# Two wide steps of the last block's quantizer put on VectorE, with a new table of due times, in a one-core perceiver kernel

## The chip, the cores and the metric

The kernel runs on one core of a Trainium2 chip. The metric is the device time of one execution in microseconds; 1745.08 us is the median of three runs of the kernel before the change. The engines are named as in the profile: PE (TensorE; its weight loads are PEld), DVE (VectorE), ACT (ScalarE), POOL (GpSimd) and SP (SyncE, which issues all DMAs here).

## What is computed

Two perceiver layers on 128 batches of 32 latent tokens of width 256, with a context of 257 tokens per batch, in f32:

```python
x = x + cross_attention(ctx, layernorm(x))            # 257 context tokens
x = x + gated_scan(layernorm(x))                      # 16 states x 512 channels, over 32 tokens
x = x + ternary_mlp(layernorm(x))                     # 256 -> 1024 -> 256, weights -1, 0, 1
x = x + focused_linear_attention(layernorm(x), ctx)   # 16 heads
x = x + latent_attention(layernorm(x))                # 16 heads, decay by distance
x = x + bitlinear_mlp(layernorm(x))                   # the quantized MLP
```

The last line is the one that the change touches. Both of its layers quantize their input by rows to 8 bits:

```python
def activation_quant(x):
    scale = 127.0 / clip(max(abs(x), axis=-1), EPS, None)
    return clip(round(x * scale), -128, 127) / scale
def bitlinear(x, w, b):
    xn = rmsnorm(x)
    return einsum('bsi,oi->bso', activation_quant(xn), weight_quant(w)) + b
# the MLP: bitlinear(gelu(bitlinear(x, w1, b1)), w2, b2), 256 -> 1024 -> 256
```

## The kernel before

**Tiles and stages.** Four batches make a group: 128 rows (4 x 32 tokens) of 256 columns, one tile `x`. The 32 groups are dealt into nine blocks, `BLOCKS = (2, 4, 4, 4, 4, 4, 4, 4, 2)` (line 1507). For each block the code records, in this order: per group the context stage (`context_group`, line 993: cross attention, then keys and values of the linear attention: `pkey`, `ku`, `ks`, `pval`, `vf`, `pk`); for the block the scan stage (`scan_block`, line 1155); and per group the latent stage (`latent_group`, line 1469: `mlp`, `linear`, `attention`, `quantized_mlp`).

**The scan stage** works on up to four groups at once (128 x 512) or two (128 x 256, in the first and the last block). It has four chunks of channels. A chunk begins with two projections `pproj` on PE, an ACT step `some` and a DVE step `pproj<-pproj,b_in,dl`; then come 16 states, each with an exponential `a` on ACT, a scan `h<-a,pproj` on DVE, and a weighted sum `acc` on DVE or, for some of the states, `h` and `some` on POOL. When the four chunks are done, `pout` on PE and `x<-pout,x` on DVE end the stage for each group.

**The quantized MLP** (line 1439) of a group: normalize (`xn`), row maximum `amax`, first quantizer, transpose (`pqT`, copied by ACT to `qT`), product `phq` with w1, scale and bias on DVE into `hq` (two halves), GELU on ACT, row maximum `amax` of `hq` on DVE, squares on ACT (`junk`, sum to `msq`), second quantizer, transpose, product `poq` with w2, and `x<-poq,dq,x` on DVE; SP writes the rows out.

**The quantizer** (line 1409) forms `rms` (a scale step and a power on POOL), `top`, its reciprocal and `qm` on DVE and the factor `dq` on POOL. Then come two steps on the whole tile: the scaling, which multiplies by `qm` and adds a large constant that rounds to an integer, in place (`hq<-hq,qm` or `xn<-xn,qm`), and the rounding, which takes the constant off again and writes bf16 (`q<-hq` or `q<-xn`). In the second quantizer (n = HID = 1024) both steps run on POOL, lines 1424 to 1427. In the first (n = 256) the scaling runs on DVE and the rounding on POOL.

**What sets the order.** Nothing runs where the code stands. A `Recorder` (line 267) notes every operation with the engines that it could run on; `order` (line 403) then plans all of them, and `trace` (line 566) issues them in the planned order, so nearly every instruction of the program has line 575 in the profile, and tiles tell them apart. Each group of operations has a pair in the table `DUE` (line 1510, 251 pairs): the due times of its first and last operation, in units of one block; `R.part()` and `R.begin()` start a new pair. The planner walks through time with the estimated costs of `ns_of` (line 42). Of the operations that can start within `WINDOW` ns of the first, it takes on each engine the one that is due first. `AHEAD` puts DMAs earlier, `SOONER` puts readers of PSUM earlier, `HORIZON` limits how far ahead of the earliest due operation a new buffer may be opened, and `PRICE` weighs the engines where an operation may run on several (copies, casts, `relu`). The planner also assumes that a POOL operation on tensors and a DVE operation of some forms (a wide `tensor_scalar` outside PSUM among them) don't run at the same time:

```python
            locks = engine == "gpsimd" and len(ins) > 0
            ...
                locks = len(tensors) > 1 if two else fast and len(tensors) > 0 and n > 64
```

Where PE has a planned gap of over 600 ns, `keep_busy` (line 553) puts in filler matmuls (`onesb,identb`, line 562), whose results are not used.

Of the kernel before, what the change touches and what calls it, by code (L numbers as in the profile page):

```python
# [12 lines left out]
ALU = mybir.AluOpType  # L13
# [3 lines left out]
P = 128  # L17
D = 256
# [569 lines left out]


GAP, FILL = 600.0, 0.7  # L590
PRICE = {"tensor": 0.0, "vector": 20.786091, "scalar": 1.959533, "gpsimd": 3.101899, "sync": 0.0}
WINDOW = 13.816
SOONER = 0.066
AHEAD = 0.777235
HORIZON = 1.581593


@with_exitstack
def perceiver_kernel(ctx: ExitStack, tc: tile.TileContext, t: dict, out: bass.AP):
# [806 lines left out]
        R.vector.tensor_tensor(xg, py[:, 0:D], xg, ALU.add)  # L1406


    def quantize(h, n, ms, k, amax, gamma):

        rms = tiny("rms", [P, 2])
        R.gpsimd.tensor_scalar(rms, ms.to_broadcast([P, 2]), k, 1e-6, ALU.mult, ALU.add)
        R.gpsimd.tensor_tensor(rms, rms, halves[:, 1:3, 0], ALU.pow)
        top = tiny("top", [P, 1])
        R.vector.tensor_scalar(top, rms[:, 0:1], 1e-5, amax, ALU.mult, ALU.max)
        m = tiny("qm", [P, 1])
        R.vector.reciprocal(m, top)
        R.vector.tensor_scalar(m, m, 127.0, None, ALU.mult)  # L1420
        worth = tiny("dq", [P, 1])
        R.gpsimd.tensor_scalar(worth, top, rms[:, 1:2], gamma, ALU.mult, ALU.mult)

        engine = R.gpsimd if n == HID else R.vector
        engine.tensor_scalar(h, h, m, ROUND, ALU.mult, ALU.add)
        q = (t2k if n == HID else t1k)([P, n], f"q{n}", BF16)
        R.gpsimd.tensor_scalar(q, h, -ROUND, 1.0, ALU.add, ALU.mult)
        return q, worth

    def transposed_ints(q, n):  # L1430
# [5 lines left out]
        R.scalar.copy(qT, pt[:, 0:n])  # L1436
        return qT

    def quantized_mlp(xg):
        xn, mv, r = norm(xg)  # L1440
        R.gpsimd.tensor_tensor(xg, xg, b2, ALU.add)
        amax = tiny("amax", [P, 1])
# [1 line left out]

        msq = tiny("msq", [P, 1])
        R.gpsimd.tensor_scalar(msq, mv[:, 1:2], r, r, ALU.mult, ALU.mult)
        q, dq = quantize(xn, D, msq, 1.0, amax, g1)
        qT = transposed_ints(q, D)
        hid = t4k([P, HID], "hq")
        for k in range(2):  # L1450
# [8 lines left out]
        junk = t2k([P, HID], "junk", BF16)  # L1459
        msq2 = tiny("msq2", [P, 1])  # L1460
        R.scalar.activation(junk, hid, AF.Square, accum_out=msq2)
        q2, dq2 = quantize(hid, HID, msq2, 1.0 / HID, amax2, g2)
        qT2 = transposed_ints(q2, HID)
        po = bank("poq")
        with R.together():
            accumulate(po[:, 0:D], [(qT2[:, c * P : (c + 1) * P], w2[:, c, :]) for c in range(8)])
        R.vector.scalar_tensor_tensor(xg, po[:, 0:D], dq2, xg, ALU.mult, ALU.add)

    def latent_group(xg, kvc, rows_out):
        mlp(xg)  # L1470
        R.part()
        linear(xg, kvc)
        R.part()
        attention(xg)
        R.part()
        quantized_mlp(xg)
        R.sync.dma_start(rows_out, xg)


# [1 line left out]
    for i, size in enumerate(BLOCKS):  # L1481
# [13 lines left out]
        for g in range(size):  # L1495
            n = n0 + g
            R.begin("l")
            latent_group(x[g], kvc[g], out[n * P : (n + 1) * P, :])
        n0 += size
    R.trace(tc)  # L1500

# [6 lines left out]


DUE = (  # L1510
    (-1.0, -0.7651), (0.1, 0.598373), (-1.116179, -1.019716), (-0.267211, 0.164717),
    (0.144, 0.184841), (0.213655, 0.218655), (0.394, 0.426463), (0.439863, 0.48282),
    (0.532341, 1.432341), (0.5, 0.607991), (0.607991, 0.869596), (0.869596, 1.1312),
    (1.1312, 1.392805), (1.39625, 1.657855), (1.65441, 1.696152), (1.574, 1.896954),
    (1.896954, 2.121576), (2.121576, 2.355619), (2.406412, 2.76275), (1.72375, 2.046704),
    (2.046704, 2.271326), (2.271326, 2.556162), (2.556162, 2.995629), (0.61878, 0.663036),
    (0.663036, 0.769121), (0.894, 0.920109), (0.927339, 0.989925), (1.167588, 1.172588),
    (1.172588, 1.241114), (1.394, 1.432573), (1.432573, 1.525039), (1.502252, 1.54223),
    (1.614935, 1.874087), (1.968546, 2.13324), (2.13324, 2.392392), (2.392392, 2.651545),
    (2.651415, 2.69787), (2.574, 2.896954), (2.896954, 3.121576), (3.222754, 3.50759),  # L1520
    (3.406412, 3.76275), (2.72375, 3.047077), (3.047077, 3.271959), (3.271959, 3.557125),
    (3.557125, 3.913875), (2.8735, 3.196454), (3.196454, 3.421076), (3.421076, 3.705912),
    (3.705912, 4.06225), (3.02325, 3.346204), (3.346204, 3.482831), (3.570826, 3.855662),
    (3.855662, 4.212), (1.644, 1.68374), (1.68374, 1.779), (1.979937, 2.019938),
    (2.019938, 2.115825), (2.140124, 2.178549), (2.178549, 2.270656), (2.424535, 2.429535),
    (2.429535, 2.55775), (2.500109, 2.615044), (2.615044, 2.874196), (2.874087, 3.13324),
    (3.13324, 3.392392), (3.392392, 3.651545), (3.651545, 3.698), (3.574, 3.896954),
    (3.896954, 4.121576), (4.121576, 4.406412), (4.406412, 4.76275), (3.72375, 4.046704),
    (4.046704, 4.271326), (4.264978, 4.556162), (4.556162, 4.9125), (3.8735, 4.196454),
    (4.196454, 4.421076), (4.421076, 4.705912), (4.631254, 4.987592), (4.02325, 4.609143),  # L1530
    (4.32519, 4.570826), (4.515235, 4.800071), (4.855662, 5.212), (2.636204, 2.676672),
    (2.676672, 2.773677), (2.886204, 2.925944), (2.925944, 3.021204), (3.147975, 3.187715),
    (3.187715, 3.282975), (3.386204, 3.431648), (3.396284, 3.505216), (3.422175, 3.53711),
    (3.536298, 3.79545), (3.79545, 4.054603), (4.054603, 4.313755), (4.392392, 4.651545),
    (4.651545, 4.698), (4.574, 4.896954), (4.896954, 5.121576), (5.121576, 5.406412),
    (5.406412, 5.76275), (4.72375, 5.046704), (5.046704, 5.271326), (5.271326, 5.556162),
    (5.556162, 5.9125), (4.702612, 5.025566), (5.196454, 5.421076), (5.421076, 5.705912),
    (5.705912, 6.06225), (5.02325, 5.346204), (5.346204, 5.570826), (5.570826, 5.855662),
    (5.855662, 6.212), (3.636204, 3.66871), (3.66871, 3.746629), (3.886204, 3.925944),
    (3.925944, 4.021204), (4.136204, 4.175136), (4.081628, 4.26846), (4.386204, 4.425944),  # L1540
    (4.425944, 4.521204), (4.521056, 4.554079), (4.627973, 4.890743), (4.874087, 5.156898),
    (5.13324, 5.392392), (5.392392, 5.651545), (5.651545, 5.698), (5.574, 5.896954),
    (5.896954, 6.121576), (6.121576, 6.406412), (6.406412, 6.76275), (5.722633, 6.045587),
    (6.045587, 6.270209), (6.270209, 6.555045), (6.555045, 6.911383), (5.8735, 6.196454),
    (6.196454, 6.421076), (6.421076, 6.705912), (6.705912, 7.06225), (6.02325, 6.346204),
    (6.301902, 6.526524), (6.570826, 6.855662), (6.855662, 7.212), (4.636204, 4.690083),
    (4.675944, 4.771204), (4.886204, 4.927641), (4.927641, 5.02697), (5.144, 5.201758),
    (5.201758, 5.340209), (5.394, 5.431974), (5.431974, 5.523), (5.5, 5.614935),
    (5.614935, 5.874087), (5.874087, 6.13324), (6.13324, 6.392392), (6.392392, 6.651545),
    (6.651545, 6.656545), (6.562991, 7.045242), (6.896954, 7.121576), (7.149964, 7.4348),  # L1550
    (7.406412, 7.76275), (6.72375, 7.046704), (7.046704, 7.271326), (7.271326, 7.556162),
    (7.518889, 7.875227), (6.8735, 7.196454), (7.196454, 7.446346), (7.421076, 7.705912),
    (7.705912, 8.06225), (7.02325, 7.346204), (7.346204, 7.570826), (7.53102, 7.815856),
    (7.855662, 8.212), (5.644, 5.684109), (5.684109, 5.780254), (5.894, 5.934222),
    (5.934222, 6.030635), (6.144, 6.163717), (6.183398, 6.277838), (6.394, 6.433837),
    (6.433837, 6.529331), (6.5, 6.614935), (6.614935, 6.874087), (6.874087, 7.13324),
    (7.13324, 7.392392), (7.392392, 7.651545), (7.651545, 7.698), (7.574, 7.904724),
    (7.896954, 8.121576), (8.121576, 8.406412), (8.406412, 8.76275), (7.72375, 8.046704),
    (8.046704, 8.271326), (8.271326, 8.556162), (8.556162, 8.9125), (7.941126, 8.26408),
    (8.196454, 8.482611), (8.421076, 8.705912), (8.701924, 9.058262), (8.02325, 8.251634),  # L1560
    (8.231279, 8.289197), (8.575174, 8.956992), (8.790837, 9.147175), (6.67874, 6.682632),
    (6.682632, 6.756779), (6.894, 6.93374), (6.93374, 7.029), (7.144, 7.18372),
    (7.18372, 7.278932), (7.422476, 7.462216), (7.462216, 7.557476), (7.501224, 7.553756),
    (7.553756, 7.685065), (7.685065, 7.816374), (7.860101, 7.991409), (7.947682, 8.078991),
    (7.995258, 8.100224), (8.130098, 8.453052), (8.393585, 8.746432), (8.618207, 8.903043),
    (8.903043, 9.259381), (8.369442, 8.664825), (8.664825, 8.870271), (8.870271, 9.13079),
    (9.13079, 9.456707), (8.222592, 8.545546), (8.582878, 8.8075), (8.802406, 9.087242),
    (9.092336, 9.39624), (8.380895, 8.732628), (8.732628, 8.95725), (8.95725, 9.242086),
    (9.242086, 9.598424), (7.644, 7.682997), (7.682997, 7.776475), (7.894, 7.93374),
    (7.93374, 8.029), (8.027527, 8.076377), (8.124824, 8.181667), (8.165022, 8.314484),  # L1570
    (8.366433, 8.49925), (8.732164, 8.864981), (8.847172, 8.866054), (8.489793, 8.799099),
    (8.733373, 8.957995), (9.049952, 9.177105), (8.969544, 9.442262), (8.255137, 8.578091),
    (8.559023, 8.723782), (8.443238, 8.947841), (8.98058, 9.391686),
)


# [75 lines left out]
```

## Time and profile before

| | |
|---|---|
| three runs, us | 1745.08, 1747.30, 1744.87; median 1745.08 |
| the profiled execution, us | 1747.35 |
| its span, first to last instruction, us | 1745.60 |
| mean granted clock | 0.987 |
| instructions | 45752 |
| PE filler matmuls, by the built program | 172 |

The profile shows one execution. Instructions are grouped by tiles (buffer numbers left out, output ahead of the arrow); the columns are the busy time of the group and the mean time of one, then the idle time of the engine just before them and what ended it. A view by stage gives the busy time of each engine between two times. The chain of waits goes back from the last instruction, at each step to what released it.

### The profile page before, as it was taken

The page shows a single profiled execution, that of the slowest core. Times are in us where ns is not written, and L with a number is a line of the kernel's source. Part 1 is how long each engine was busy: PE and PEld are TensorE (multiplying, and loading weights), DVE is VectorE, ACT ScalarE, POOL GpSimd, SP SyncE. Part 2 cuts the span into 40 slices and gives each one's busy share as a digit, 9 for nine tenths or more (in the row PEclk, how much of TensorE's full clock was granted, in tenths as well). Part 3 has the DMA queues.
Part 4 walks back from the last instruction along what each step waited for, and adds up shares of the span by engine and source line. Part 5 has one row for each costly group of instructions (what it writes and reads, how often), then busy time and mean ns, then how long its engine had stood idle before and what let it go on. Part 6 is the DMA issues. An engine that isn't in the chain of part 4 may idle for free.

```text
span 1745.6 us, 45752 instructions
## 1 busy us (share of the span) xinstructions
PE 1657.3 (95%) x17523; PEld 1203.7 (69%) x17591; DVE 1508.2 (86%) x2956; ACT 1426.8 (82%) x3495; POOL 1356.6 (78%) x2145
## 2 busy tenths in 40 slices
PE   8999999999999999999999999999999988888996
PEld 5777777776776777767777677776777665656663
DVE  5479689989988999988999799979999899988866
ACT  3677698889987999879887989888888898777665
POOL 4766758678776988778788779867888799878887
PEclk9999999999999999999999999999999999999998
DMA  7312000111000011001110021001110000000000
GB/s 221 107 45 86 29 29 29 45 41 32 10 29 29 8 64 38 29 2 41 35 35 29 8 62 41 29 2 35 41 35 29 4 23 1 7 1 2 8 8 19
DMA packets 44762, 59.74 MB, mean 34 GB/s; under 512 B 8704, under 2 KB 27008, under 8 KB 44544
## 3 DMA queue, kind: packets, MB, share of 16 engines
q1 hardware_dynamic: 44544, 56.81, 10.1%
q8 instruction: 139, 2.28, 0.6%
q14 instruction: 79, 0.65, 0.1%
HBM read 52.32 MB, written 4.19 MB: 32 GB/s over the span
## 4 chain that ended last, share of the span: by engine, by line
PE 39%; DVE 28%; ACT 14%; POOL 13%; issue 4%; DMA 0%; DVEq 0%; POOLq 0%; ACTq 0%
DVE h L575 13%; PE pval L575 6%; DVE acc L575 6%; PE pkey L575 6%; PE pproj L575 4%; ACT a L575 3%; PE pT L575 3%; POOL ku L575 2%; POOL rstd L575 2%; ACT ks L575 2%; PE pqa L575 2%; PE pmlp L575 2%; ACT L575 2%; PE pk L575 2%; DVE st L575 2%
## 5 line engine op out<-in xcount | busy, mean ns | idle before, releaser
L575 DVE TENSOR_TENSOR_SCAN h<-a,pproj 128x512 f32<-128x512 f32 (+1 forms) x576 | 613.3, 1086 | 22.4 <-ACT a L575 17.6
L575 ACT ACTIVATE a<-dl,a_neg 128x496 f32<-128x496 f32 (+1 forms) x576 | 366.8, 664 | 71.3 <-DVE h L575 68.4
L575 DVE SCALAR_TENSOR_TENSOR acc<-h,w_st,acc 128x512 f32<-128x512 f32 (+1 forms) x436 | 299.5, 687 | 0.6
L575 PE MATMUL pval<-wkv,cT 128*128 128x256 f32 x1024 | 245.5, 386 | 1.4 <-DVE y L575 1.3
L575 PE MATMUL pkey<-wkv,cT 128*128 128x256 f32 x1024 | 238.1, 386 | 0.0
L575 ACT ACTIVATE ks<-ku 128x256 f32<-128x256 f32 x512 | 209.0, 415 | 16.8 <-POOL ku L575 15.5
L575 PEld LDWEIGHTS pkey<-wkv,cT 128*128 128x128 f32 x1024 | 189.3, 190 | 38.0 <-issue 14.9
L575 PEld LDWEIGHTS pval<-wkv,cT 128*128 128x128 f32 x1024 | 188.9, 191 | 31.4 <-issue 2.8
L575 POOL TENSOR_TENSOR ku<-ku,e 128x512 f32<-128x512 f32 x128 | 162.7, 1281 | 33.9 <-ACT ku L575 28.3
L575 POOL TENSOR_TENSOR ku<-ks,ku 128x512 f32<-128x512 f32 x128 | 165.4, 1300 | 18.7 <-ACT ks L575 17.8
L575 POOL TENSOR_TENSOR kn<-kn,halves 128x4 f32<-128x4 f32 x128 | 131.1, 1026 | 24.4 <-ACT ks L575 23.4
L575 POOL TENSOR_TENSOR rstd<-rstd,halves 128x1 f32<-128x1 f32 x224 | 125.8, 565 | 7.3
L575 ACT ACTIVATE vf<-pval,kf 128x256 f32<-128x256 f32 x256 | 107.4, 472 | 23.2 <-PE pval L575 15.5
L575 ACT ACT_TABLE_LOAD x95 | 121.9, 1283 | 1.7
L575 PE MATMUL pproj<-xTs,w_in 128*128 128x512 f32 (+1 forms) x288 | 122.4, 552 | 0.3
L575 POOL TENSOR_SCALAR rstd<-mv 128x1 f32<-128x1 f32 x224 | 45.2, 202 | 96.6 <-DVE mv L575 73.2
L575 POOL TENSOR_TENSOR some<-some,h 128x512 f32<-128x512 f32 (+1 forms) x104 | 115.1, 1107 | 2.8
L575 PE MATMUL pmlp<-w_pr,hT 128*128 128x256 f32 x512 | 116.7, 381 | 0.0
L575 PEld LDWEIGHTS pmlp<-w_pr,hT 128*128 128x128 f32 x512 | 95.6, 190 | 13.8 <-issue 0.8
L575 ACT ACTIVATION_READ_ACCUMULATOR ks<-ku 128x1 f32 x512 | 100.6, 196 | 0.0
L575 POOL TENSOR_SCALAR h<-h,w_st 128x512 f32<-128x512 f32 (+1 forms) x104 | 65.3, 630 | 40.7 <-DVE h L575 35.5
L575 PE MATMUL ph<-w_fc,x 128*128 128x512 bf16 x350 | 89.2, 379 | 5.3 <-ACT ku L575 1.4
(291 smaller groups left out, 3883.7 us busy)
## 6 DMA issues: line engine op xcount, KB each, us to landing
cx<-in_ctx_dram SPq DMA_DIRECT2D x64, 512.0 KB
x<-in_x_dram SPq DMA_DIRECT2D x32, 128.0 KB
cr<-in_ctx_dram SPq DMA_DIRECT2D x128, 32.0 KB
out_dram<-x SPq DMA_DIRECT2D x32, 128.0 KB
vlz<-vl SPq DMA_DIRECT2D x128, 1.1 KB
w_in<-in_w_inT_dram SPq DMA_DIRECT2D x1, 1024.0 KB
raw_fc<-in_w_fcT_dram SPq DMA_DIRECT2D x2, 512.0 KB
raw_pr<-in_w_prT_dram SPq DMA_DIRECT2D x2, 512.0 KB
```

Source lines behind the costliest of these rows:

```text
L575: ins = getattr(engine, name)(*(traced(a) for a in args), **{k: traced(v) for k, v in kw.items()}).ins
```

## The change

The last block's two groups run the scaling and the rounding of their second quantizer on DVE instead of POOL; the first quantizer and all other blocks stay as they were. The five numbers of the planner and all but 2 of the 251 pairs of `DUE` change (their starts by 0.03 of a block in the median). The diff without the rest of the table:

```diff
-PRICE = {"tensor": 0.0, "vector": 20.786091, "scalar": 1.959533, "gpsimd": 3.101899, "sync": 0.0}
-WINDOW = 13.816
-SOONER = 0.066
-AHEAD = 0.777235
-HORIZON = 1.581593
+PRICE = {"tensor": 0.0, "vector": 28.013093, "scalar": 4.356996, "gpsimd": 3.720234, "sync": 0.0}
+WINDOW = 13.821085
+SOONER = 0.0675
+AHEAD = 0.744939
+HORIZON = 1.665209
...
-    def quantize(h, n, ms, k, amax, gamma):
+    def quantize(h, n, ms, k, amax, gamma, late):
...
-        engine = R.gpsimd if n == HID else R.vector
+        wide = R.vector if late else R.gpsimd
+        engine = wide if n == HID else R.vector
         engine.tensor_scalar(h, h, m, ROUND, ALU.mult, ALU.add)
         q = (t2k if n == HID else t1k)([P, n], f"q{n}", BF16)
-        R.gpsimd.tensor_scalar(q, h, -ROUND, 1.0, ALU.add, ALU.mult)
+        engine = wide if n == HID else R.gpsimd
+        engine.tensor_scalar(q, h, -ROUND, 1.0, ALU.add, ALU.mult)
...
-            latent_group(x[g], kvc[g], out[n * P : (n + 1) * P, :])
+            latent_group(x[g], kvc[g], out[n * P : (n + 1) * P, :], i == len(BLOCKS) - 1)
...
 DUE = (
-    (-1.0, -0.7651), (0.1, 0.598373), (-1.116179, -1.019716), (-0.267211, 0.164717),
-    (0.144, 0.184841), (0.213655, 0.218655), (0.394, 0.426463), (0.439863, 0.48282),
+    (-1.233024, -0.335498), (0.019828, 0.480193), (-1.629912, -0.869437), (-0.837897, -0.738361),
+    (-0.093681, -0.088914), (-0.021839, -0.017211), (0.306149, 0.488484), (0.39917, 0.543159),
...
```

`late` is handed down through `latent_group` and `quantized_mlp`. In the built program the work stays nearly the same and its order changes everywhere: four wide steps move from POOL to DVE, 11 casts of `x<-xT` from ACT to POOL, and the fillers go from 172 to 168. At the start, SP issues the first group's `x`, `cx` and `cr` ahead of the weights `wv`, `w_in` and `w_gate`, where they stood behind them.

## The prediction

> **What bounds the kernel now.** I read the page first, then the busy time by stage, then the chain of waits of the last 32 us, and last the rows of the moved steps. Busy shares, from the page:
>
> ```profile
> PE 1657.3 (95%) x17523; PEld 1203.7 (69%) x17591; DVE 1508.2 (86%) x2956; ACT 1426.8 (82%) x3495; POOL 1356.6 (78%) x2145
> DVE   5479689989988999988999799979999899988866
> ```
>
> Four engines work most of the time, so no single sum sets the span. DVE is nearly full from the seventh slice to the thirty-seventh and loose at both ends. Cut at the first scan (98.9 us), at the start of the last one (1622.2) and at the last `x<-pout` (1640.0):
>
> ```profile
> 0.00:98.90 98.90, 93.18 (x790) 69.26 (x791) 43.00 (x114) 49.77 (x161) 57.72 (x108) 0.97 0.48 146
> 98.90:1622.20 1523.30, 1464.62 (x15389) 1064.94 (x15448) 1377.45 (x2590) 1299.05 (x3181) 1202.54 (x1867) 0.99 0.09 29
> 1640.00:1745.60 105.60, 83.66 (x1150) 57.99 (x1154) 71.59 (x208) 67.22 (x132) 83.34 (x149) 0.92 0.04 13
> ```
>
> Columns: window, its length, then busy PE, PEld, DVE, ACT, POOL, clock, DMA. The reader is to see three regimes. The front is PE's (93 of 99 us). The middle is DVE's: 1377.45 of 1523.30, 90.4%. In the end no engine is full, and POOL is the busiest (83.34 of 105.60). The last chain says what the end waits for:
>
> ```profile
> 1729.68 1.10 POOL hq L575
> 1730.78 0.32 POOL dq L575
> 1731.11 1.09 POOL hq L575
> ...
> 1732.56 1.05 POOL q L575
> 1733.60 0.67 POOL rms L575
> 1734.28 1.04 POOL q L575
> 1735.36 1.03 PE pqT L575 x8
> ```
>
> From 1714.09 to 1735.36 that chain hardly leaves POOL: several groups are in their quantizers at once, and their small `rms` and `dq` steps queue between 1 us wide steps.
>
> **The moved steps.** Of 32 groups only the last block's two change engine; that is two scalings `hq<-hq,qm` and two roundings `q<-hq`.
>
> ```profile
> L575 POOL TENSOR_SCALAR hq<-hq,qm x32: 1111/1118/1249, 372.7 to 1735.6; 128x1024 f32<-128x1024 f32 x32
> L575 POOL TENSOR_SCALAR q<-hq x32: 1040/1047/1052, 374.3 to 1736.8; 128x1024 bf16<-128x1024 f32 x32
> L575 DVE TENSOR_SCALAR neg_w<-raw_w,thr x4: 726/746/1768, 133.9 to 165.8; 128x1024 f32<-128x1024 f32 x4
> L575 DVE TENSOR_SCALAR w_out<-w_out x1: 686/686/686, 28.3 to 28.3; 128x1024 f32<-128x1024 f32 x1
> ```
>
> POOL loses 2 x (1.118 + 1.047) = 4.33 us. DVE has no row for either step. The nearest for the scaling is neg_w (same shape, one pointer scalar), 0.746; for the rounding w_out (no pointer, but f32 out instead of bf16), 0.686. So DVE gains 2 x 1.432 = 2.86 us, and one pair is 0.73 us shorter in its own chain.
>
> The relief has a catch in the neg_w row: its maximum is 1.768. That one started at 165.81 while POOL's `ku<-ks,ku` ran, 1.0 us over the median. The `ku` step, begun 0.08 us after an earlier neg_w, took 1.798 us where its group's mean is 1.300: 0.50 more. So either engine's wide step can delay the other. Best case: the steps run side by side and POOL is relieved of all 4.33. By the row, each DVE step costs POOL 0.50: 4.33 - 4 x 0.50 = 2.33. Worst: POOL's relief is hidden by other work and the 2.86 lie on the path, +2.9. I take -2.3, since that row is the same shape beside a wide POOL step, as here.
>
> The Trainium skill speaks against the change here ("SBUF — State Buffer", section "SBUF: two separate sides"): VectorE in a two-port mode and GpSimd lock one port pair for a whole instruction, the loser blocks. As an estimate from it, POOL would lose the whole DVE time of 2.86, and the relief would be 1.47, not 2.33. The two delays above show its direction, not its full length.
>
> **The new table.** All but 2 of its 251 pairs change, so the order of the whole kernel moves. The instructions hardly do: compared by engine and tile, 11 casts `x<-xT` go from ACT (0.405 each) to POOL (0.397), so ACT -4.5 and POOL +4.4; filler matmuls go from 172 to 168; the ACT table loads stay 96. POOL's total is then level (+4.4 - 4.3).
>
> To see what the new order does, I summed each engine's instructions in either built order up to a mark, each at its group's mean busy time in this trace:
>
> ```
> DVE work, us              before   after
> ahead of the first scan     42.0    46.5
> between first and last    1381.4  1373.8
> behind the last scan        84.8    90.8
> behind the last x<-pout     68.2    77.1
> behind the last x<-pya      17.2    22.7
> other engines: ACT behind the last a 76.7 -> 82.0
> POOL behind the last x<-x,s 76.7 -> 81.8; PE behind the last pout 79.5 -> 88.3
> ```
>
> *Front.* SP issues x, cx and cr ahead of wv, w_in and w_gate (1.75 MB), three issues of some 0.5 us earlier. The first context transposes and scores now stand on PE in the stretch where before ran fillers while DVE worked through `sp_y`. But PE's work ahead of the first projection is 86.0 -> 87.4, and it was busy 93 of 99 us. I take 0, with 5 us off as the end: the pieces of the chain that move there are `pT` 0.43, `pq` 1.71, `pcT` 1.02 + 0.87 and `psc` 1.01 us, which stood on it from 23 to 35 us. No loss: of the moved weights wv is first used at 45 us, the others at 92. What counts is that 4.5 us of DVE work slip ahead of the first scan, where DVE idled.
>
> *Middle.* DVE has 7.6 us less between first and last scan. At 90.4% that is 8.4 us.
>
> *End.* More stands behind the last scan on every engine: DVE +6.0, of which 2.9 are the moved steps. From 1622.2 to the end took 123.4 us. If the stretch is set by dependences, the work fits into the idle time: 0. If DVE's share stays as it was, it grows to 123.4 x 90.8/84.8 = 132.1: +8.7. PE has 30 fillers there instead of 12, at a clock that was 0.79 from 1714 on; I count nothing for that. POOL's load gives a similar +7 (81.8/76.7 of 105.6). I take the middle, +4.4.
>
> Sum: -8.4 + 4.4 - 2.3 = -6.3 us. The profiled execution took 1747.35 (span 1745.60, 1.75 around it), the median of three runs is 1745.08, so this execution is 2.3 us slow. On its own time the sum gives 1741.0; on the median 1738.8. I forecast **1739**.
>
> Ends of the sum: -5 - 8.4 + 0 - 4.3 = -17.7, so 1727; and -8.4 + 8.7 + 2.9 = +3.2, so 1748.
>
> **Rivals.**
> *The end takes back what the middle gives.* The work is only pushed past the last scan: -8.4 + 8.7 - 2.3 = -2.0, time 1743. For it: POOL's 79% in the end, and its solid chain. Against: DVE is only 68% busy there (71.59 of 105.60), and these groups were late because they waited. Within 0.2% of 1745.08 (3.5 us, about what a measurement of this kernel can tell from no change).
>
> *Slower: the block starts lose their cover.* Each block begins with projections that wait for the previous stage; DVE then waits for ACT's `some`:
>
> ```profile
> L575 DVE SCALAR_TENSOR_TENSOR pproj<-pproj,b_in,dl 128x512 f32<-128x512 f32 x28 | 21.1, 752 | 36.8 <-ACT some L575 36.7
> ```
>
> With the two-group blocks that is 43.7 us. What DVE can do there is what stands between the previous scan and this `pproj`. Summed over the eight later blocks, that cover falls from 72.9 to 64.6 us in the new order (10.4 to 2.3 at the sixth block alone). If every lost microsecond becomes idle, +8.3, and the end pays its +8.7 too: -8.4 + 8.7 + 8.3 = +8.6, with the relief hidden; time 1754. It decides once the idle time before `pproj` grows by 9.8 us (-6.3 + 9.8 = +3.5), or by 5.5 where the end pays in full. Against it: at four of the eight starts the wait was under 0.3 us, with covers of 6.4 to 16.3; at the other four it was 6 to 10 us with covers of 5.5 to 10.4. So cover is only part of it.
>
> *The change does not do what it says:* DVE's steps hold POOL up so that the relief is gone or reversed. Price: +2.3 to +5.2 on the forecast, 1741 to 1744. It shows as wide steps of 1.5 us or more.
>
> **Chances.** Forecast, with its neighbours to 1741.6: 0.60. End takes it back, or the locked steps, within 0.2%: 0.16. Slower by over 0.2%: 0.24, mostly lost cover. The range runs from 1729 to 1754: it takes in nearly all down to the lower end of the sum, and the slower rival, and leaves out some 2 in 10.
>
> **What would show it.** Front: first scan near 98.9 us or up to 4 earlier. Middle: last scan starting near 1614 rather than 1622.2, DVE busy about 1374 between the two. Steps: four DVE rows 128x1024 of 0.7 to 0.8 us; 1.2 or more means they meet POOL. End: last `x<-pout` near 1633, the time from there to the end 103 to 108 us (105.6 before), and POOL no longer solid from 1714 to 1735. It is wrong if the last scan starts no earlier than 1619, or if the stretch behind it grows by more than 8 us; and the slower rival is right if the idle time before `pproj` passes 53 us.

## The result, and the profile after

| | before | after |
|---|---|---|
| median, us | 1744.97 (1743.05 to 1747.30, 4 runs) | 1716.75 (1713.78 to 1719.02, 4 runs) |
| ratio | | 0.9837 [0.9817, 0.9857] |
| the profiled execution, us | 1747.35 | 1715.90 |
| its span, us | 1745.60 | 1714.20 |
| mean granted clock | 0.987 | 0.996 |

The change made the kernel faster by 28.2 us. The forecast was 1739 and the range ran from 1729 to 1754: the sign was right, the size far too small. Blocks are numbered from 0 to 8 from here on.

The changed kernel's page, the row of busy times and the row of DVE in 40 slices:

```profile
PE 1650.3 (96%) x17587; PEld 1200.9 (70%) x17587; DVE 1501.8 (88%) x2960; ACT 1422.8 (83%) x3484; POOL 1362.6 (79%) x2152
DVE  5389699988997997959998997979999899999777
```

DVE has four instructions more (the moved steps) and yet 6.4 us less busy time; its last slices read 99999777, where they read 99888866. The stretches of the changed kernel, cut at the same events (first scan 96.5, start of the last scan 1590.3, last `x<-pout` 1606.7); columns as before: window, length, busy PE, PEld, DVE, ACT, POOL, clock, DMA:

```profile
0.00:96.50 96.50, 91.33 (x820) 68.27 (x824) 48.50 (x119) 50.83 (x161) 61.29 (x108) 1.00 0.54 161
96.50:1590.30 1493.80, 1455.50 (x15264) 1058.83 (x15260) 1358.92 (x2575) 1289.02 (x3153) 1201.18 (x1869) 1.00 0.09 29
1606.70:1714.20 107.50, 87.92 (x1244) 61.33 (x1242) 79.91 (x227) 73.59 (x143) 86.52 (x151) 0.98 0.04 13
```

The reader is to see that nearly all of the gain stands in the second row: 1523.30 us became 1493.80. DVE's work there fell by 18.5 us (1377.45 to 1358.92), its idle time by 11.0 (145.85 to 134.88). Up to the first scan 2.4 us were won, although DVE does 5.5 us more there (43.00 to 48.50). From the start of the last scan to the end hardly anything changed (123.4 and 123.9 us).

The moved steps, rows of the changed kernel; min/median/max duration in ns, first and last start:

```profile
L575 POOL TENSOR_SCALAR hq<-hq,qm x30: 1111/1117/1131, 358.0 to 1705.3; 128x1024 f32<-128x1024 f32 x30
L575 POOL TENSOR_SCALAR q<-hq x30: 1042/1046/1355, 359.2 to 1706.6; 128x1024 bf16<-128x1024 f32 x30
L575 DVE TENSOR_SCALAR hq<-hq,qm x2: 735/978/1221, 1700.4 to 1704.5; 128x1024 f32<-128x1024 f32 x2
L575 DVE TENSOR_SCALAR q<-hq x2: 684/1069/1454, 1703.5 to 1705.6; 128x1024 bf16<-128x1024 f32 x2
```

Two of the four took 0.735 and 0.684 us, the other two 1.221 and 1.454. The end of the changed kernel's chain of waits (start, length, what):

```profile
1700.37 1.06 ACT hq L575
1701.46 1.15 ACT junk L575 x2
1702.61 0.91 ACT qT L575
1703.56 1.05 PE poq L575 x8
1704.61 0.46 PE pqT L575 x8
1705.09 1.02 ACT qT L575
1706.16 1.05 PE poq L575 x8
```

From 1693.5 us on no POOL step is left in it (further ahead, from 1682 us, it still runs through POOL); where the old chain went through POOL's `hq` and `q` of 1.1 us, it now goes from ACT to PE and back. And DVE's wait for `some` at the starts of the chunks, by its two rows in the changed kernel, is 28.9 + 2.8 = 31.7 us instead of 43.7:

```profile
L575 DVE SCALAR_TENSOR_TENSOR pproj<-pproj,b_in,dl 128x512 f32<-128x512 f32 x28 | 21.1, 752 | 28.9 <-ACT some L575 28.9
L575 DVE SCALAR_TENSOR_TENSOR pproj<-pproj,b_in,dl 128x256 f32<-128x256 f32 x8 | 3.9, 482 | 2.8 <-ACT some L575 2.8
```

### The profile page after: what moved, and what is told of

Its sections match the earlier page's. It is cut to its first block, busy times and chain, and to the rows that moved or that the text cites. A ratio compares the mean times of both kernels' runs of the same rounds, so it can differ in the third digit from the quotient of the medians.

```text
span 1714.2 us, 45797 instructions
## 1 busy us (share of the span) xinstructions
PE 1650.3 (96%) x17587; PEld 1200.9 (70%) x17587; DVE 1501.8 (88%) x2960; ACT 1422.8 (83%) x3484; POOL 1362.6 (79%) x2152
## 4 chain that ended last, share of the span: by engine, by line
PE 48%; DVE 24%; ACT 15%; POOL 10%; issue 3%; DMA 0%; DVEq 0%; POOLq 0%; ACTq 0%; SPq 0%
DVE h L575 10%; PE pkey L575 7%; PE pproj L575 7%; PE pval L575 6%; DVE acc L575 5%; PE pT L575 3%; PE pmlp L575 3%; PE pqa L575 3%; POOL ku L575 3%; ACT a L575 2%; PE pk L575 2%; ACT ks L575 2%; ACT L575 2%; PE pka L575 2%; PE pcT L575 2%
```

## The experiments

The theory after the result: the moved steps are worth some 3 us; the rest is the new order, and it wins at the places where one stage hands over to the next, not by the amount of work. The rivals: the gain is spread over all blocks; it needs the whole new table; or it is the last part alone. Most of the kernels below issue one plan's order up to a mark and the other plan's order from there:

```diff
-        for i in self.order():
+        for i in self.spliced():
...
+        head = first[: ends[CUT - 1] + 1]
...
+        rest = [i for i in second if i not in done]
```

`first` and `second` are the two full plans, each made with its own table and its own five numbers. Of `rest`, the first operation whose inputs are issued and whose buffers are free is taken. `ends` are the `x<-pout` steps: the 2nd ends block 0's scan stage, the 26th block 6's; the 28th is the second of block 7's four. (The expectations call it the end of the eighth block's scan stage; the 30th is that.) All ratios are against runs of the kernel before on the same chip; a gain in us is the ratio's distance from 1 times 1745.

**The steps alone.** The changed kernel with the old table and numbers:

```diff
-PRICE = {"tensor": 0.0, "vector": 28.013093, "scalar": 4.356996, "gpsimd": 3.720234, "sync": 0.0}
+PRICE = {"tensor": 0.0, "vector": 20.786091, "scalar": 1.959533, "gpsimd": 3.101899, "sync": 0.0}
...
 DUE = (
-    (-1.233024, -0.335498), (0.019828, 0.480193), (-1.629912, -0.869437), (-0.837897, -0.738361),
+    (-1.0, -0.7651), (0.1, 0.598373), (-1.116179, -1.019716), (-0.267211, 0.164717),
```

> The four wide steps of the last block on DVE, with the table and the planner's numbers of before; the order is that of before up to the last few instructions. Theory A (the gain is the new order's, made where block 0 and the last block run): 1743 to 1745 us, the relief of POOL worth 0 to 2 us. Theory B (the relief of POOL at the end is a good part of it): 1740 or less. Theory C (the steps lock each other out and cost): 1746 or more. Of before's 32.0 us from the last x<-pya to the end, A expects 30 to 32, B under 29.

Measured: 0.9983 [0.9974, 0.9991], 3.0 us [1.6, 4.5] faster, between theories A (0 to 2) and B (5 or more). The time from the last `x<-pya` to the end went from 31.6 to 28.4 us, as B expected. The four DVE steps took 0.816, 0.694, 0.754 and 0.685, together 2.95 us; only the first met a wide POOL step, for 0.27 us.

**The table alone.** The changed kernel with the steps back on POOL:

```diff
-            latent_group(x[g], kvc[g], out[n * P : (n + 1) * P, :], i == len(BLOCKS) - 1)
+            latent_group(x[g], kvc[g], out[n * P : (n + 1) * P, :], False)
```

> The new table and numbers, all wide steps on POOL as before. Theory A: 1716 to 1719 us, last scan start near 1590 us as in after. Theory B: 1721 or more, and the stretch behind the last x<-pout longer than after's 107 us by 4 or more.

Measured: 0.9851 [0.9837, 0.9865], 26.0 us, so 1719 by the ratio (its median of 1721.85 stands beside 1747.17 for the kernel before on that chip): theory A, at its slow end. The stretch behind the last `x<-pout` took 110.4 us, 2.9 more than after the change. Nine tenths of the gain are the order's, and 3.0 + 26.0 is about the whole, 28.4 by its ratio. The profiled execution of this kernel, whose lines are shown below, was the fastest of its four: 1717.41 us at clock 0.997, where the others took 1721.8 to 1723.0 at 0.991 or 0.992.

**The new order up to the end of block 0's scans** (`FIRST` new, `SECOND` old, `CUT = 2`).

> Order spliced: the new plan's order up to the second x<-pout (end of block 0's scan stage), then all that is left in the old plan's order; steps on POOL. Theory A (the gain is made in block 0 and in the last block, little between): 1745 minus 10 to 15, so 1730 to 1735, and the second x<-pout near 195 us. Rival D (the gain is a better order throughout, 1.6% of every stretch): a front of 200 us is worth 3 us, so 1740 to 1743. Rival E (a lead gained early is lost again, because DVE is full later): 1743 to 1746 although the second x<-pout comes near 195.

Measured: 0.9945 [0.9930, 0.9961], 9.6 us, just under theory A's 10 to 15 and three times rival D's 3. In 11% of the span a third of the gain is made.

**The new order from the 28th `x<-pout`** (`FIRST` old, `SECOND` new, `CUT = 28`).

> Order spliced the other way: the old plan's order up to the end of the eighth block's scan stage (the 28th x<-pout, 1517 us in before), then the new plan's order for what is left; steps on POOL. Theory A: 1745 minus 13 to 18, so 1727 to 1732, with some 105 us between the 28th and the last x<-pout instead of 123. Rival D: the last 230 us are worth 4 us, 1740 to 1742. Rival E: the stretch to the last x<-pout shrinks and the one behind it grows as much, 1743 to 1746.

Measured: 1.0012 [1.0002, 1.0023], nothing won: rival E. The stretch from the 28th to the last `x<-pout` shrank from 126.3 to 119.1 us, and the one behind it grew from 105.2 to 112.8. From the 28th `x<-pout` to the end it took 232.0 us, as in the kernel before (231.5); the changed kernel takes 215.4 and the table alone 215.6 for the same part. DVE's idle time from that mark to the end of the last scan shows the difference: 16.0 us here (103.40 - 87.38), 5.5 with the table alone (89.40 - 83.94). In the kernel before it was 15.5, in the changed kernel 7.8. The kernel with the cut, the table alone, then the kernel before and the changed one:

```profile
1515.20:1618.60 103.40, 86.19 (x850) 58.74 (x849) 87.38 (x222) 79.43 (x176) 81.42 (x140) 0.95 0.01 3
```

```profile
1499.80:1589.20 89.40, 80.58 (x840) 55.84 (x839) 83.94 (x219) 74.64 (x167) 80.58 (x137) 1.00 0.01 3
```

```profile
1514.10:1622.90 108.80, 93.16 (x1000) 64.02 (x1002) 93.34 (x233) 81.68 (x188) 88.16 (x151) 0.95 0.01 4
```

```profile
1498.80:1590.90 92.10, 83.36 (x840) 57.36 (x839) 84.28 (x218) 74.72 (x167) 80.38 (x137) 0.96 0.01 3
```

So the same order of the last part is worth some 15 us or nothing, by the state in which it is entered (231.5 us before, 215.6 with the table alone, and 216.4 in the kernel cut at the 26th step, below).

**The new order up to the 28th `x<-pout`** (`FIRST` new, `SECOND` old, `CUT = 28`).

> The new plan's order up to the second x<-pout of the ninth-from-first scan stage's predecessor, that is the 28th x<-pout step (1498.8 us in the changed kernel, 1514.1 in the one before), then exactly the remaining operations in the old plan's order; all quantizers as before the change, on POOL. Theory 'the gains add': the new order of the last part alone brought nothing from the old state (1.2 us slower), so the old order of that part costs nothing here either: the whole lead of 15.3 us at the 28th x<-pout survives, less the 3 us of the moved steps that are not in this kernel: 1730 us. Rival 'the lead is given back, because the old order of the last part was made for the old state': the stretch from the 28th x<-pout to the end, 231.5 us before, grows by half the lead or more: 1737 to 1745 us. Rival 'the new middle needs the new end': the old order has to wait for work that the new order had put off, slower than before, 1746 us or more.

Measured: 0.9931 [0.9911, 0.9951], 12.0 us. The lead at the mark, 15.7 us, survives but for 2.4: the stretch behind it took 233.9. The old end loses little, and gains nothing, although this kernel has 6 of the last block's 64 scans ahead of the 28th step, as the changed one has (the kernel before has none). DVE is idle for 20.1 us from there to the end of the last scan:

```profile
1498.40:1609.20 110.80, 93.13 (x994) 63.36 (x991) 90.67 (x229) 78.05 (x179) 87.70 (x148) 0.95 0.01 4
```

Against the kernel with the cut behind block 0, blocks 1 to 7 bring 12.0 - 9.6 = 2.4 us, within the two intervals of nothing.

**The old order through block 0, then the new** (`CUT = 2`).

> The old plan's order up to the second x<-pout step (209.6 us before), then the remaining operations in the new plan's order; all quantizers as before the change, on POOL. Front and block 0 alone brought 9.6 us, the moved steps alone 2.9, the whole change 28.2. Theory 'the gains add': 28.2 - 9.6 - 2.9 = 15.7 us faster, about 1729 us. Rival 'the middle gains only because it is entered earlier with more work done ahead': the new order of the middle, entered from the old state, brings less than 6 us: 1739 us or more.

Measured: 0.9933 [0.9912, 0.9953], 11.7 us, between the two theories: adding foretold 15.7, just outside the interval, and the rival less than 6. The front's gain and the rest add up to 9.6 + 11.7 + 3.0 = 24.3 of 28.4 us.

**Without the fillers into `ph`**, in the kernel before:

```diff
-        if min(out.buf.ops) != op.n or out.dtype != F32:
+        if min(out.buf.ops) != op.n or out.dtype != F32 or out.buf.name == "ph":
```

> The kernel before, without the filler matmuls that PE runs into the output tiles of the quantized and ternary MLPs' first product (ph). In the last block of the kernel before 21 of them (6.1 us of PE) stand between the last two scan stages, and two runs of them lie on the chain of waits at 1535 and 1541 us (3.99 and 1.73 us); the new order has 5 there (1.5 us). Theory 'the fillers delay PE's real work in the last block, and the new order gains by having fewer': the last scan starts 4 to 6 us earlier, time 1739 to 1741. Rival 'they fill gaps that are there anyway': within 2 us of before. Rival 'they keep the granted clock up': the clock falls below 0.987 after the gaps and the time rises by 2 us or more.

Measured: 0.9977 [0.9966, 0.9988], 4.0 us faster, the first theory at its lower end; the mean clock is 0.988 as before (0.987). Only the ternary MLP's first product has a tile of this name (the quantized one's is `phq` and keeps its fillers). 28 fillers go, 172 to 144, and 21 of them stood between the last two scan stages. The last scan ends 3.6 us earlier (1622.9 to 1619.3); the 28th `x<-pout` (1514.1 and 1513.9) and the time behind the last one (105.2 in both) stay. Fillers that stand on the chain cost time, and the new order has 5 of them in this place instead of 21.

**The new pairs with the old numbers** (only `PRICE` to `HORIZON` as before).

> The new table of pairs with the five old planner numbers, all quantizers as before the change. Table and numbers together brought 26 us. Theory 'the pairs carry the gain, the numbers moved by a few per cent only': 1722 to 1732 us. Rival 'pairs and numbers are one tuned set': the plan has 264 fillers instead of 172 and 168, that is some 95 more planned gaps of PE over 0.6 us, about 0.6 us each or more, so that 57 us of planned idle time come back, of which a third or more shows: 1745 us or later, slower than before.

Measured: 1.0282 [1.0258, 1.0307], 49 us slower. The rival is right: a table of due times is worth what it is worth only with the numbers it was made with. Block 0 still gains (its scans end at 198.1 instead of 209.6 us); the loss comes behind it.

**The old order through block 6, then the new** (`CUT = 26`).

> The old plan's order up to the 26th x<-pout step (1392.9 us before; block 7's scan stage lies behind it), then the remaining operations in the new plan's order; all quantizers as before the change, on POOL. From the 28th x<-pout on, the new order brought nothing when entered from the old state (232.0 us to the end, 231.5 before) and 16 us when entered from its own (215.5). The new order ends block 7's scan stage with 6 or 7 of the last block's 64 scans already done; the old one with none. Theory 'the last block gains because its first chunk of channels, with its projections, is begun beneath block 7's scans, so that DVE finds work where it waited 3.84 us for the first pproj and 4.86 us for a den step': here block 7 is in the new order too, and the stretch from the 28th x<-pout to the end falls to 216 to 220 us, the time to 1731 to 1736. Rival 'the state is built up over several blocks': the stretch stays at 226 us or more, time 1741 or more.

Measured: 0.9960 [0.9945, 0.9976], 7.0 us. The stretch from the 28th `x<-pout` fell to 216.4 us, as with the table alone: what the last block needs can be made from the end of block 6's scan stage on. The whole time is just past the slow end of what was expected, since block 7's own part, from the 26th to the 28th step, took 125.1 us instead of 121.2; the early chunk now lies in it, and DVE does 2.0 us more there.

**The early chunk held back**, in the table alone:

```diff
+            if late and size == 2 and ic == 0:
+                R.held.update(range(start, len(R.ops)))
...
-        head = first[: ends[CUT - 1] + 1]
+        head = [i for i in first[: ends[CUT - 1] + 1] if i not in self.held]
```

> The new plan's order with one thing altered: the operations of the last block's first chunk of channels (projections, exponentials, scans, sums) that the new plan issues ahead of the 28th x<-pout step are taken out there and issued right behind it; all quantizers as before the change, on POOL (the table alone gave 1721.9). Theory 'this early chunk is what makes the last block short': the 28th x<-pout comes some 5 us earlier (6 scans and their sums less ahead of it), and the waits for pproj and den of some 4 to 5 us each come back, with the chunk's own 10 us of dependent start: the stretch from there to the end grows from 215.5 to 228 to 233 us, the time by 6 to 12 us to 1728 to 1734. Rival 'the early chunk is only order, the same work is done a little later': what the stretch grows by is won ahead of it, time within 3 us of 1722.

Measured: 0.9938 [0.9921, 0.9955], 10.8 us faster than before, that is 15.2 [11.4, 19.0] slower than the table alone (26.0) by the two ratios, and 13.6 by the two profiled executions: more than the 6 to 12 expected, though the interval reaches into them. The 28th step came 3.5 us earlier (1496.3), of which 1.9 were there at the 26th already; the rest took 232.7 us instead of 215.6. The decisive lines are DVE's instructions around that step; [idle <- what ended it] at the end. First with the chunk held back, then the table alone:

```profile
1494.11 0.42 DVE L641 TENSOR_TENSOR x<-pout,x 128x256 f32<-128x256 f32 x1 [1.44 <-PE pout L641]
1495.84 0.42 DVE L641 TENSOR_TENSOR x<-pout,x 128x256 f32<-128x256 f32 x1 [1.30 <-PE pout L641]
1501.60 0.49 DVE L641 SCALAR_TENSOR_TENSOR pproj<-pproj,b_in,dl 128x256 f32<-128x256 f32 x1 [5.33 <-ACT some L641]
1502.12 1.26 DVE L641 TENSOR_TENSOR_SCAN h<-a,pproj 128x256 f32<-128x256 f32 x2
```

```profile
1494.82 0.49 DVE L575 SCALAR_TENSOR_TENSOR pproj<-pproj,b_in,dl 128x256 f32<-128x256 f32 x1 [0.23 <-ACT some L575]
...
1495.61 1.83 DVE L575 TENSOR_TENSOR_SCAN h<-a,pproj 128x256 f32<-128x256 f32 x3
1497.36 0.40 DVE L575 TENSOR_TENSOR x<-pout,x 128x256 f32<-128x256 f32 x1
1497.68 1.83 DVE L575 TENSOR_TENSOR_SCAN h<-a,pproj 128x256 f32<-128x256 f32 x3
1499.42 0.40 DVE L575 TENSOR_TENSOR x<-pout,x 128x256 f32<-128x256 f32 x1
```

In the lower view the last block's scans stand between block 7's four `x<-pout` steps, so DVE has work while PE makes each `pout`, and the last block's first `some` (1494.2 us) comes ahead of them. It does not run beneath block 7's scans, as was expected: the last of these ended at 1483.0. In the upper view DVE waits 1.44 and 1.30 us for `pout` and 5.33 for `some`, 8.1 in all. From that mark to the end of the last scan DVE is then idle for 16.2 us instead of 5.5, as in the kernel with the cut there (16.0).

This shows that the new order needs the chunk, not that the kernel before lost its time at this hand-over. There other work of DVE lies between the `x<-pout` steps, and its waits are short:

```profile
1516.81 0.42 DVE L575 TENSOR_TENSOR x<-pout,x 128x256 f32<-128x256 f32 x1 [0.56 <-PE pout L575]
...
1518.27 0.49 DVE L575 SCALAR_TENSOR_TENSOR pproj<-pproj,b_in,dl 128x256 f32<-128x256 f32 x1 [0.29 <-ACT some L575]
```

Its 15.5 us of idle time in the stretch lie elsewhere, the longest wait being one of 3.29 us at 1613 us (`ea` for POOL's `some`).

**The new order up to the first scan** (the cut at that scan, then the old order).

> The new plan's order up to the first scan (97.2 us in the changed kernel, 98.9 to 99.6 before), then exactly the remaining operations in the old plan's order; all quantizers as before the change, on POOL. With the cut at the second x<-pout step, behind block 0's scan stage, 9.6 us were won. Theory 'the gain is made in the front: the 4.5 us of DVE work put ahead of the first scan, where DVE idles, and 2 us of the scan's start': 5 to 8 us faster, 1738 to 1741. Rival 'it is made inside block 0, where DVE idles 9.3 us in the old order and 3.8 in the new': 0 to 3 us faster, 1742 or more.

Measured: 0.9971 [0.9962, 0.9980], 5.1 us. With 9.6 for the cut behind block 0, the front makes 5.1 and block 0's scan stage 4.5 [1.4, 7.6]; each theory had half of it. The work ahead of the first scan is the front's part (DVE 48.46 us there instead of 43.00). Of block 0's part the cut behind block 0 shows where it is: its stretch from the first scan to the second `x<-pout` is 98.90 us at clock 1.00, with DVE idle for 3.8, against 110.70, 0.97 and 9.3 in the kernel before. (With the cut at the first scan it is 106.90 at 0.98, with 11.2 idle for nearly the same DVE work, 95.70.) The two stretches, cut behind block 0 first, then before:

```profile
96.50:195.40 98.90, 98.84 (x1040) 77.64 (x1033) 95.13 (x202) 81.71 (x254) 78.67 (x112) 1.00 0.19 59
```

```profile
98.90:209.60 110.70, 106.00 (x1129) 83.18 (x1128) 101.37 (x207) 84.52 (x260) 75.90 (x113) 0.97 0.19 61
```

3.7 of the 9.3 us are two waits of `xn<-x,mv,rstd` for POOL's `rstd`, at 203 and 206 us, where block 0 hands over to block 1; they are 3.7 with the cut at the first scan too, and 0.0 with the cut behind block 0.

**The new order up to the last `x<-pout`, then the old**, with the steps on DVE (`CUT = 32`). This was to be a kernel faster than both.

> The changed kernel, with its own quantizers (four wide steps on DVE), in the new plan's order up to the 32nd and last x<-pout step (1606.7 us in the changed kernel), then the remaining operations in the old plan's order. Behind that step the changed kernel takes 107.5 us, the old order with the moved steps 102.0, the old order without them 105.2. Theory 'the new order of the end is simply the worse one': the old order takes 102 us there from the new state too, 5 us faster than the changed kernel, about 1711 us. Rival 'the end is longer because more work is left for it': DVE has 79.9 us of work behind that step instead of 71.2, and the old order does not lessen it: within 2 us of the changed kernel's 1716.8. Rival 'the old order fits this state badly, as in the last block': 1719 us or more.

Measured: 0.9890 [0.9873, 0.9906], 19.2 us faster than before and 9.2 slower than the changed kernel. The third theory is right: behind the last `x<-pout` it took 118.8 us instead of 107.5. The stretch to its end, from 1.9 us ahead of that step:

```profile
1606.70:1727.40 120.70, 92.22 (x1237) 63.47 (x1235) 81.74 (x234) 70.71 (x139) 87.65 (x157) 0.90 0.04 11
```

DVE has about the work that the changed kernel has there (81.74 and 79.91): what is longer is its idle time, at clock 0.90 instead of 0.98. The old order that took 102.0 us from its own state is a bad one from another.

The lead over the kernel before can be read from the traces without fixing on one event: sum DVE's instructions in their order, each at its group's mean over all shapes in the kernel before, and compare the times at which the same amount of work is done. In us:

```
DVE work done, us          100    180    600   1200   1400   1440   1500   the span
reached before at          133    188    624   1247   1453   1492   1540   1745.6
lead of: changed kernel    8.0   11.4   14.6   13.7   19.9   17.9   23.1   31.4
new until first scan       3.5    5.0    5.2    5.7    5.7    5.7    5.8    7.9
new until block 0          8.0   11.4    9.3    9.4    9.4    9.1    9.0    9.5
new until 28th pout        8.3   11.7   14.9   13.9   20.1   18.1   13.8   13.3
first chunk held           8.8   12.1   15.4   14.8   20.9   18.9   14.4   16.6
new from block 7          -0.7   -0.9   -0.7   -0.5    0.3   -1.7    3.5   10.8
```

The changed kernel has 11.4 us by the time block 0 is done, 14.6 and 13.7 in the middle columns, and 19.9 by 1453 us. The orders differ inside a block, so a lead rises and falls by some us between columns; only differences between kernels are to be read. The kernel with the chunk held back and the one that goes over to the old order at the 28th `x<-pout` follow the changed one to 1492 us and fall back by 4 us within the next 50, while it goes on to 23.1. The second of them has the early scans: the chunk pays only with the order that follows it.

## Why the prediction was wrong, point by point

**What bounds the kernel: right, but drawn too coarsely.** DVE is full in the middle: 90.4% before, 91.0% after. But the idle time does not go with the work: it fell by 11.0 us where 7.6 us less work at a fixed share would take off 0.8. Part of it sits at the hand-overs between stages, as DVE's waits for `some` (43.7 to 31.7 us) and for `rstd` (3.7 to 0.0 behind block 0) show, and an order can remove it.

**Front, 0 with 5 off as the end.** The first scan came 2.4 us earlier, and the 4.5 us of DVE work that the summed orders put ahead of it were there (5.5 by the windows). The cut at the first scan gives 5.1 us for both. The mechanism was the one named, and so was the size: the prediction booked the 4.5 us under the middle, where they are 5.0 of the 8.4.

**Middle, "At 90.4% that is 8.4 us": this is the step that failed.** It measured 29.5. The rule made the order worth only the work that it moves out of the stretch, at a fixed share of idle time. It missed two things of nearly the same size. DVE's busy time there fell by 18.5 us where 7.6 were counted, and its idle time by 11.0 where the rule leaves 0.8. Of the 18.5 us, 5.5 now stand ahead of the first scan, 2.5 behind the start of the last one (87.80 to 94.39, less 4.1 for the moved steps), and 10.5 are gone from the whole kernel. By the marks, the 29.5 are 11.8 in block 0 (110.7 to 98.9), 1.1 between the second and the 28th `x<-pout` (1304.5 to 1303.4), and 16.7 between the 28th and the end of the last scan (108.8 to 92.1; 9.1 less work and 7.6 less idle time). What the experiments and traces show of it:
- The last block's early chunk, 15.2 us [11.4, 19.0] when held back out of the new order. The two built orders showed it before any run: of the last block's 64 scans 6 stand ahead of the 28th `x<-pout` in the new order and none in the old. Sums of work between the first and the last scan can't see it, since the chunk lies between these marks in either order. It is not enough alone: with the old order behind it nothing was won.
- Block 0's scan stage, 4.5 us [1.4, 7.6], in which the two waits at the hand-over to block 1 (3.7 us) are gone.
- DVE's steps themselves got shorter or overlapped more: the 10.5 us that are gone. By their rows `xn<-x,mv,rstd` went from 552 to 522 ns in the mean (96 times) and `acc<-h,w_st,some` of 128x512 from 829 to 782 (28 times), 4.2 us together. It goes with the order of blocks 1 to 6: `xn` took 515 to 523 ns in every kernel that has the whole new order there and 552 to 560 in every one that has the old. Of the 96 steps, 55 began while POOL was at work in the kernel before and took 661 ns in the mean, the others 406; after the change it was 49, with 598 and 442. That POOL's steps make the difference is likely by these rows; no run tested it.

**End, +4.4.** The stretch behind the start of the last scan grew by 0.5 with the relief in it; without it, +3.5 by the steps' measured 3.0. The work did stand there (DVE 79.91 behind the last `x<-pout` instead of 71.59, +8.3, counted as 8.9), and the last stretch of 107.5 us is within the 103 to 108 foretold. Near, but in part by luck: 4.4 was the middle between two rules, neither of which a run bears out, and the stretch behind the last `x<-pout` took from 102.0 to 118.8 us by the order and the state in which it was entered. The rival "the end takes back what the middle gives" is wrong only because the middle gave so much more.

**The steps, -2.3.** 3.0 [1.6, 4.5] measured alone. The worked value is inside the interval, but not by its mechanism: it let each of the four DVE steps cost POOL 0.50 us, and with the steps alone three of them met no wide POOL step. That it fits is luck in part. In the changed kernel POOL ran beside two of the DVE steps (start, length; POOL's first):

```profile
1700.00 1.04 POOL L575 TENSOR_SCALAR q<-hq 128x1024 bf16<-128x1024 f32 x1
...
1705.35 1.12 POOL L575 TENSOR_SCALAR hq<-hq,qm 128x1024 f32<-128x1024 f32 x1
1706.55 1.35 POOL L575 TENSOR_SCALAR q<-hq 128x1024 bf16<-128x1024 f32 x1
```

```profile
1700.37 1.22 DVE L575 TENSOR_SCALAR hq<-hq,qm 128x1024 f32<-128x1024 f32 x1
...
1705.56 1.45 DVE L575 TENSOR_SCALAR q<-hq 128x1024 bf16<-128x1024 f32 x1
```

If the later step waited until the earlier one was done, the first DVE step would end at 1701.04 + 0.735 = 1701.78 and the second at 1706.47 + 0.684 = 1707.15; they ended at 1701.59 and 1707.01, so the wait is nearly whole, 0.19 and 0.14 us short. With the steps alone, the one that met POOL's `q` for 0.27 us ended 0.18 us short of such a wait, only 0.08 longer than 0.735. POOL's `q` that began at 1706.55 took 0.31 more than its median, of the 0.46 us for which DVE was still at work. The Trainium skill has this as an exclusive lock held for a whole instruction ("SBUF — State Buffer", section "SBUF: two separate sides"); these rows agree with it but for 0.14 to 0.19 us. The prediction's estimate from it, a relief of 1.47 us, lies just below the measured interval; with the steps alone only one of the four met a wide POOL step. "The change does not do what it says" is therefore wrong for the time; its sign, a step of 1.5 us or more, did not appear, though 1.22 and 1.45 show two steps that met POOL.

**Slower, the block starts lose their cover: wrong.** The idle time before `pproj` fell from 43.7 to 31.7 us, where 53 was to show it. The cover was summed between the previous scan and the next `pproj`, but the new order also moves the first `some` itself. From the end of the previous stage's last scan to its start it took 136.4 us before and 122.2 after, summed over the eight later blocks: 14.2 less, more than the 8.3 of cover that were foretold to go. At block 5 alone (the prediction's sixth) it was 22.2 and 5.0.

**What stays open.** It is open how much of the difference is PE's clock. From the 28th `x<-pout` to the end of the last scan, the kernels that won nothing there ran at 0.92 to 0.95 and those that won at 0.95 to 1.00, but no kernel changed the clock alone. An estimate from the record: 21 executions of the kernel before on one chip go from 1750 us at a mean clock of 0.985 to 1745.6 at 0.989, about 1 us for each 0.001. The changed kernel's four ran at 0.992 to 0.998, 0.995 in the mean, so some 6 to 8 of the 28.2 us go with the clock. Whether the new order raised the clock, and by what, is not shown. Open too is which of its waits in the last block the new order saves the kernel before, and what in that order shortens DVE's steps. And the front's and the later gains, each alone, add up to 24.3 and not 28.4 us; the intervals, some 3 us each, allow the difference to be nothing.

## What to carry to other kernels

When a whole order changes, don't price it by the work between two marks at the old idle share. List the places where the bounding engine idles, look in both built orders at what stands on that engine during the hand-over to the next stage, and above all whether the next stage's first, dependent chain (projection, exponential, first scans) has begun before the previous one's closing steps: here the new order lost 15 us when one chunk that it begins early, 6 scans of 576 ahead of the mark, was held back. And an order is one piece: the pairs without their numbers lost 49 us, the new end without its beginning won nothing, the old end behind the new beginning lost 9.

## What the runs showed of the hardware

Filler matmuls are not free where they stand ahead of work that others wait for: without 28 of them, 21 of which (6.1 us of PE) stood in one stretch, the kernel was 4.0 us [2.1, 5.9] faster, and the granted clock did without them (0.988 against 0.987). A wide DVE `tensor_scalar` beside a wide POOL one is close to serial in both directions: 1.22 and 1.45 us where 0.735 and 0.684 are the time alone, and for a POOL step 1.355 where 1.046 is the median. Each of the three DVE steps that met one ended 0.14 to 0.19 us before the end of POOL's step and its own time alone would give.
